# A three-layer graph convolution on one core: every other chunk of layer 1 split for a one-pass product, 18 blocks instead of 16 by count matrices, and an opening that asks for x earlier and holds the first searches

## The chip, the cores and the metric

The kernel runs on one NeuronCore of a Trainium2 chip. A core has engines that run side by side, each taking its own instructions in order: TensorE (PE: matrix products, weight loads listed as PEld), VectorE (DVE), ScalarE (ACT), GpSimd (POOL) and SyncE (SP, which here only issues transfers). Transfers run on 16 DMA engines; SP, ACT and POOL can issue them. The metric is device time in microseconds (us), the median of several runs; before the change it is 2774.49 us.

## The reference

A graph has 6250 nodes with 256 features each (x) and 100,000 edges (src to dst), sorted by dst. Each node also gets an edge to itself. With deg the number of edges that arrive at a node:

```python
dinv = jnp.where(deg > 0, jax.lax.rsqrt(deg), 0.0)
norm_edge = dinv[src] * dinv[dst]
h = x
for W, b in ((W1, b1), (W2, b2), (W3, b3)):      # 256->512, 512->512, 512->256
    agg = segment_sum((h @ W)[src] * norm_edge[:, None], dst, n)
    h = relu(agg + b)
out = layernorm(x + h)
```

Everything is float32. Summing over edges and multiplying by W can change places, and the kernel sums first in layers 1 and 2 (over 256 and 512 columns) and multiplies by W3 first for layer 3 (256 columns).

## The kernel before, in words

**Blocks.** The nodes are cut into NB = 50 blocks of Q = 125. A block's edges lie in a run of the sorted list, about 2000 of them; the kernel loads CAP = 2048 places for each block, 16 for each of 128 partitions (KF = 16). What a block has beyond 2048 goes into a rest, one for each group of GRP = 10 blocks.

**Gathered blocks.** For one chunk (128 edges, one of a block's 16) POOL gathers 128 rows of the layer's table from HBM (L814), by the edges' sources. DVE makes a 0/1 matrix from the edges' targets (L783, for four chunks at once), and PE multiplies matrix and rows (L840) into a sum in PSUM. A float32 product takes two records on PE. Where a chunk is "halved", the row is split first: ACT casts it to the short form fp32r (L855), DVE subtracts that from the row (L858), and high and low part, side by side, go through PE in the short form, twice as wide. Layer 2 halves three chunks of four, layer 3 all but the rests, layer 1 none. SPLIT gives each layer's lags: a row gathered at step c is cast at c + hi_lag, subtracted at c + lo_lag and multiplied at c + lag. The rows lie in a ring of places in one big buffer, room.

**Blocks by matrices (dense).** For the first FEW = 16 blocks of layer 1 and the first MANY = 28 of layer 3 the kernel doesn't gather. It makes the matrix that counts the edges between every source and each of the block's 125 targets, and multiplies it with the whole table, which lies split in SBUF (parts): 50 products of 512 columns a block (L883), after ACT (or DVE) has turned pieces of the matrix from bytes into fp32r (L791). A matrix is made by counts(): for each of 25 groups of 5 targets DVE makes two 0/1 matrices (L684, L686), PE multiplies them (L692), and ACT copies the counts out as bytes (L676) into one buffer, made. SP stores it to HBM (kept) and loads it again (fetch) into one of two buffers, used. The last 12 matrices are made during layer 2. Where the edges of a group of targets begin is found before that by windows(t), a search for 125 groups at a time (t = 0 to 5): comparisons on DVE, two products on PE, one gather by POOL, and transposes, in slots (L614 to L667). Before, all six searches run within layer 1's steps, on a scratch part of room.

**The order of work** is written out by hand. layer() has one step for each gather (548 in layer 1: 34 blocks of 16, and 4 rests; 805 in layer 2; 355 in layer 3, plus lag). A step issues, in this order, a gather, the halving of earlier chunks, the product of an earlier chunk, one advance of every block that is being finished, the fixed extras (searches, counts), and as many dense products as the spacing asks for by then. Finishing (after1, after2, after3) and counts are generators: a number that they yield is how many steps they wait. `first` is the step from which dense products are due, and a dense block may start 10 steps after its matrix was fetched:

```python
until = min(len(dense) * NB, int((chunk + 1 - first) * NB / spacing))
...
if chunk < total - 1 and (len(there) <= m or there[m] > chunk):
    break
```

**Around the layers.** The find stage (L1146 on) loads dst, finds where each block's edges begin and, on ACT's queue, asks for the first two groups of x. The opening of sorted_path then loads the edges (SP 25 blocks, ACT 15, POOL 10), asks for the rest of x, counts degrees in three stages for each of five groups (counted: L499 to L534; DVE, PE, ACT), scales x by dinv on ACT, stores it as layer 1's table (SP), splits it into parts (L542, L543), and loads the weights (late_w, L1127). SP's and ACT's transfers take eight semaphores in turn, so that each waits for the one eight before it.

## Time and profile before

| | |
|---|---|
| runs | 2773.09, 2774.49, 2784.61 us |
| profiled execution | 2775.35 us; span of its instructions 2773.6 us |
| granted PE clock, mean | 0.908 |
| busy: PE, DVE, ACT, POOL | 78%, 52%, 43%, 62% |
| first gather of layer 1 / 2 / 3 | 85.5 / 952.5 / 2190.8 us |
| gathers of layer 1 / 2 / 3 | 548 / 805 / 355 |

The span is the time from the first to the last instruction of one execution. A group of instructions is listed as line, engine, operation, what it writes and reads, and then its busy time, the mean ns of one, and the idle time of its engine ahead of it with what ended it. A list of waits has the waiting instruction, the one that ended the wait, total us, times and the longest. "remote" and "issue" in such a place mean that the profile names no releaser. A row of the timeline has start, duration, engine and line; neighbours are merged, and matmuls overlap, so their pace is read from starts.

### The profile page before, as it was taken

To read this page: it belongs to the slowest core of one execution; us is meant where nothing else is said; L and a number is where in the kernel's file an instruction comes from. 1 tells how busy PE (TensorE), PEld (TensorE's weight loads), DVE (VectorE), ACT (ScalarE), POOL (GpSimd) and SP (SyncE) were. 2 spreads that over 40 slices of the span, in tenths; PEclk is the share of its full clock that TensorE was granted. 3 is DMA by queue.
4 is the path that set the end of the run, shared out by engine and by line. 5 is a ranking of instruction groups with operands and counts; after the bars stand their busy time and mean duration, and the time that the engine had idled before them with its cause. 6 is when DMAs were issued, how large, how long until landed. Compare 5 with 4: busy or idle time off the path is not lost.

```text
span 2773.6 us, 30036 instructions
## 1 busy us (share of the span) xinstructions
PE 2155.2 (78%) x8189; PEld 1492.7 (54%) x8189; DVE 1430.3 (52%) x3657; ACT 1179.0 (43%) x2501; POOL 1716.7 (62%) x1749
## 2 busy tenths in 40 slices
PE   3368877888888768788878777887887679888887
PEld 2246555665566435555545544554555556666664
DVE  5454443444342256556656555565555246556666
ACT  2234444444442244445544443454443245444443
POOL 2565656566666567776767666667766366666663
PEclk9889999999999879999889989998999789999998
DMA  7444545454544466676767667666676355555553
GB/s 177 127 119 136 142 118 152 119 154 123 149 121 133 125 197 197 200 211 196 210 187 212 194 175 214 190 205 192 203 208 195 95 136 148 145 144 154 144 152 95
DMA packets 179311, 450.29 MB, mean 162 GB/s; under 512 B 43801, under 2 KB 75883, under 8 KB 179132
## 3 DMA queue, kind: packets, MB, share of 16 engines
q0 software_dynamic: 108992, 330.44, 42.4%
q1 hardware_dynamic: 53735, 104.78, 13.0%
q10 hardware_dynamic: 16405, 13.06, 1.8%
q8 instruction: 66, 1.08, 0.2%
q14 instruction: 113, 0.93, 0.1%
HBM read 394.24 MB, written 53.88 MB: 162 GB/s over the span
## 4 chain that ended last, share of the span: by engine, by line
PE 35%; issue 13%; DVE 6%; ACT 4%; another core or an unknown queue 3%; DMA 3%; POOL 1%; ACTq 0%; SPq 0%; DVEq 0%; POOLq 0%
PE sacc L840 15%; PE sacc L883 11%; PE win_ps L970 4%; DVE halves L858 3%; ACT halves L855 2%; PE smm L987 2%; DMA room<-tab,ssrc 2%; PE mat_ps L692 1%; POOL room L814 1%; DVE shot L783 1%; PE szt_ps L906 1%; DVE hot_key L686 1%; ACT room L676 1%; ACT piece L791 0%
## 5 line engine op out<-in xcount | busy, mean ns | idle before, releaser
L814 POOL DMA_INDIRECT room<-tab,ssrc x1696 | 1681.5, 991 | 888.4 <-issue 329.4
L858 DVE TENSOR_TENSOR halves<-room,halves 128x512 fp32r<-128x512 f32 (+1 forms) x952 | 556.1, 590 | 617.2 <-issue 280.7
L883 PE MATMUL sacc<-parts,piece 125*125 125x512 f32 x2200 | 758.6, 444 | 61.1 <-ACT piece L791 28.6
L840 PE MATMUL sacc<-halves,shot 128*125 128x512 f32 x1552 | 655.1, 490 | 144.8 <-issue 71.9
L855 ACT CAST halves<-room 128x512 fp32r<-128x512 f32 (+1 forms) x952 | 498.5, 539 | 561.0 <-DMA room<-tab,ssrc 149.6
L840 PE MATMUL sacc<-room,shot 128*125 128x256 f32 (+1 forms) x1700 | 660.7, 477 | 33.8 <-DMA room<-tab,ssrc 32.0
L883 PEld LDWEIGHTS sacc<-parts,piece 125*125 125x125 f32 x2200 | 413.8, 197 | 297.3 <-issue 163.2
L840 PEld LDWEIGHTS sacc<-halves,shot 128*125 128x125 f32 x1552 | 295.9, 204 | 460.2 <-issue 293.9
L676 ACT CAST room<-mat_ps 125x250 uint8<-125x250 f32 x700 | 305.0, 436 | 540.7 <-PE mat_ps L692 211.6
L840 PEld LDWEIGHTS sacc<-room,shot 128*125 128x125 f32 x1700 | 329.9, 202 | 201.4 <-issue 108.5
L692 PE MATMUL mat_ps<-hot_key,hot_lo 128*125 128x250 bf16 x700 | 199.9, 286 | 287.8 <-issue 106.8
L684 DVE TENSOR_SCALAR hot_lo<-keys,slots 128x125 bf16<-128x125 bf16 x700 | 192.9, 276 | 378.8 <-PE mat_ps L692 139.4
L783 DVE TENSOR_TENSOR shot<-near_cols,sdlo 128x500 fp32r<-128x500 f32 (+1 forms) x452 | 302.7, 670 | 103.7 <-PE sacc L840 55.0
L791 ACT CAST piece<-room 125x625 fp32r<-125x625 uint8 x356 | 252.9, 711 | 148.4 <-PE sacc L883 53.4
L970 PE MATMUL win_ps<-room,w_sb 128*128 128x250 f32 x800 | 217.0, 398 | 1.6 <-ACT room L978 0.9
L686 DVE TENSOR_SCALAR hot_key<-keys,slots 128x250 bf16<-128x250 bf16 x700 | 209.7, 300 | 0.0
L970 PEld LDWEIGHTS win_ps<-room,w_sb 128*128 128x128 f32 x800 | 162.8, 204 | 51.9 <-issue 24.2
L692 PEld LDWEIGHTS <-hot_lo 128*125 128x125 bf16 x700 | 101.7, 146 | 85.9 <-issue 34.9
L930 PE MATMUL smm<-w,szt 128*125 128x512 f32 x200 | 108.8, 632 | 7.5 <-issue 6.5
L987 PE MATMUL smm<-w,room 128*125 128x256 f32 x400 | 108.5, 397 | 0.0
L987 PEld LDWEIGHTS smm<-w,room 128*125 128x125 f32 x400 | 79.3, 198 | 26.6 <-issue 12.8
L814 POOL DMA_INDIRECT room<-tab,rest x12 | 14.1, 1178 | 109.1 <-DMA sb<-in_L_gnn_b 57.6
(162 smaller groups left out, 973.0 us busy)
## 6 DMA issues: line engine op xcount, KB each, us to landing
room<-kept SPq DMA_DIRECT2D x44, 683.6 KB
room<-tab,ssrc POOLq DMA_INDIRECT x1696
kept<-room SPq DMA_DIRECT2D x28, 683.6 KB
tab<-st SPq DMA_DIRECT2D x75, 224.0 KB
room<-tab SPq DMA_DIRECT2D x50, 224.0 KB
room<-in_x SPq DMA_DIRECT2D x50, 112.0 KB
out<-st ACTq DMA_DIRECT2D x50, 112.0 KB
room<-in_x ACTq DMA_DIRECT2D x4, 1120.0 KB
```

The source lines that it names most:

```text
L676: nc.scalar.copy(made[:, :, u * G:(u + 1) * G], mat_ps[:Q, u % 2, :G * NB].rearrange("p (k r) -> p k r", r=G))
L686: nc.vector.tensor_scalar(hot_key, keys, slots[:, t, 1, w:w + 1], None, op0=ALU.is_equal)
L692: nc.tensor.matmul(mat_ps[:Q, u % 2, :G * NB], lhsT=hot_lo, rhs=hot_key, start=True, stop=True)
L783: nc.vector.tensor_tensor(hot[:, :n], near_cols.unsqueeze(1).to_broadcast([P, n, Q]), dlo.rearrange("p b j -> p (b j)")[:, at:at + n].unsq ...
L791: convert(piece, used[m % 2][:, c * PIECE:(c + 1) * PIECE, :])
L814: nc.gpsimd.indirect_dma_start(out=row, out_offset=None, in_=tables[i], in_offset=bass.IndirectOffsetOnAxis(ap=at, axis=0))
L840: nc.tensor.matmul(acc[:Q, :size], lhsT=hot, rhs=row[:, c0:c0 + size], start=(i == 1 and k == c0 == 0), stop=(k == KF and c0 + size == row ...
L855: nc.scalar.copy(halves[:, :width], landed[chunk - hi_lag])
L858: nc.vector.tensor_sub(halves[:, width:], landed.pop(chunk - lo_lag), halves[:, :width].bitcast(F32))
L883: nc.tensor.matmul(acc_d[:Q], lhsT=got[done // PIECE][:, k % PIECE, :], rhs=parts[:, k], start=False, stop=(k == NB - 1))
L970: nc.tensor.matmul(h_ps[:, f, :], lhsT=w2_sb[:, k, (f2 + f) * P:(f2 + f + 1) * P], rhs=zt2[:, k, :], start=(k == 0), stop=(k == KH - 1))
L987: nc.tensor.matmul(u_ps[:, h, :], lhsT=ht2[:, k, h * Q:(h + 1) * Q], rhs=w3_sb[:, k, :], start=(k == 0), stop=(k == KH - 1))
```

## The change

1. Layer 1 splits every other chunk (`items[c][2] % 2 > 0`: 8 of 16) with the lags (1, 2, 4), from a new pool of three buffers.
2. FEW goes from 16 to 18: layer 1 gathers 32 blocks, and layer 2 makes 10 matrices instead of 12. Dense products are due from step 28 instead of 52. counts() no longer takes two of its steps in one step of the layer now and then (only the first matrix does, every other time), and its last copy is one step of its loop.
3. The scratch of the searches moves from room to w2's place in SBUF, and layer 1's ring of rows grows from 12 to 19. w2 is loaded at the start of layer 2, ahead of w3, instead of in the opening.
4. The opening: three groups of x instead of two are asked for in the find stage. One group is left to ACT, and SP takes the last group and the zero rows. The first two searches run between the stages of counted and the splitting of x; the other four stay in layer 1.
5. after1 waits two steps more in two places. Layer 3's dense sums use one bank of their own and the two banks of the searches and matrices, instead of three of their own.

windows() itself is unchanged and only stands further up in the file, ahead of the opening that now uses it. The diff, cut to its core:

```diff
-SPLIT = (None, (1, 2, 4), (3, 4, 6))
-FEW = 16
+SPLIT = ((1, 2, 4), (1, 2, 4), (3, 4, 6))
+FEW = 18
...
+    scratch = w2_sb.rearrange("p k n -> p (k n)")
...
-            for g in range(2 * GRP, 4 * GRP, GRP):
-                load_x(nc.scalar, rows_of(room, g), g)
-            load_x(nc.scalar, last_x, NB - GRP)
+            load_x(nc.scalar, rows_of(room, 3 * GRP), 3 * GRP)
+            load_x(nc.sync, last_x, NB - GRP)
             for table in tables:
-                nc.scalar.dma_start(out=table[N:N + 1, :], in_=zero[:, :table.shape[1]])
+                nc.sync.dma_start(out=table[N:N + 1, :], in_=zero[:, :table.shape[1]])
...
+            nc.vector.tensor_copy(thr0, thr_i)
+            nc.vector.tensor_copy(own0, own_i)
+            first_windows = (step for t in range(2) for step in windows(t))
             stages = [counted(g) for g in range(0, NB, GRP)]
             for k in range(NG + 2):
                 for g in range(max(0, k - 2), min(k + 1, NG)):
                     next(stages[g])
+                    if k > 0:
+                        next(first_windows, None)
             nc.vector.tensor_copy(src, ed[:, :, :, 0])
             for g in range(0, NB, GRP):
                 in_parts(g)
+                next(first_windows, None)
+                next(first_windows, None)
+            for _ in first_windows:
+                pass
             late_w()
...
-    scratch = room[:, 3 * MW:3 * MW + 1856]
-    first_rows = [room[:, at:at + C] for at in range(3 * MW + 1856, room.shape[1] - C + 1, C)]
+    first_rows = [room[:, at:at + C] for at in range(3 * MW, room.shape[1] - C + 1, C)]
...
+    split = one.enter_context(tc.tile_pool(name="sfirst_split", bufs=3))
...
+    def dense_bank(i, m):
+        if i < 2:
+            return ps_acc.tile([P, HID], F32, name="sacc")
+        if m % 3 == 0:
+            return ps_dense.tile([P, HID], F32, name="sacc")
+        if m % 3 == 1:
+            return ps_mat.tile([P, HID], F32, name="win_ps")
+        return ps_mat.tile([P, 2, 256], F32, name="mat_ps").rearrange("p t n -> p (t n)")
...
-    def counts(b, rush=GB + 2):
+    def counts(b, rush=GB + 3):
...
-        for u in range(GB + 2):
+        for u in range(GB + 3):
...
-            if u > 1:
+            if 1 < u < GB + 2:
...
-        yield 1
-        moved(GB - 1)
-        yield SOON
         by_rows(nc.sync, made.rearrange("p k v -> p (k v)"), kept[b], store=True)
...
-        hi_lag, lo_lag, lag = SPLIT[i] or (0, 0, 0)
+        hi_lag, lo_lag, lag = SPLIT[i]
...
-            return 0 <= c < total and items[c][1] is not None and (i == 2 or i == 1 and items[c][2] % 4 > 0)
+            return 0 <= c < total and items[c][1] is not None and (i == 2 or items[c][2] % (2, 4)[i] > 0)
...
-                        acc_d = ps_dense.tile([P, HID], F32, name="sacc")
+                        acc_d = dense_bank(i, m)
...
-        yield SOON
+        yield SOON + 2
         yield from transposed(zs, C, got)
...
-        yield SOON
+        yield SOON + 2
         yield from take("mm2", 1)
...
-    seen = 0
+    seen = 2
...
-        for t in range(NW):
-            yield from quick(windows(t)) if t == 0 else windows(t)
+        for t in range(seen, NW):
+            yield from windows(t)
             seen += 1
...
-            yield from counts(b, 5)
+            yield from counts(b) if m else counts(b, 2)
...
-    first = 52
+    first = 28
...
     def last_weights():
+        load_w2()
         load_w3()
         yield 1
...
-    ps_dense = ctx.enter_context(tc.tile_pool(name="sps_dense", bufs=3, space=bass.MemoryType.PSUM))
+    ps_dense = ctx.enter_context(tc.tile_pool(name="sps_dense", bufs=1, space=bass.MemoryType.PSUM))
...
-            for g in range(0, 2 * GRP, GRP):
+            for g in range(0, 3 * GRP, GRP):
                 load_x(nc.scalar, rows_of(room, g), g)
```

## Prediction

> **What bounds the kernel now.** I read the windows first, one for each stage, cut where the gathers (POOL L814) of a layer begin and end. Columns: stretch and length, then busy time (and instructions) of PE, weight loads, DVE, ACT and POOL, the granted clock, DMA share and GB/s.
>
> ```profile
> 85.50:166.00 80.50, 41.99 (x148) 26.67 (x149) 36.11 (x119) 13.02 (x31) 55.24 (x54) 0.86 0.35 99
> 166.00:475.00 309.00, 242.29 (x1032) 176.86 (x1032) 142.31 (x515) 132.04 (x293) 188.20 (x197) 0.93 0.47 133
> 475.00:828.00 353.00, 289.59 (x1214) 211.16 (x1213) 144.31 (x491) 152.96 (x334) 219.14 (x231) 0.94 0.47 136
> 828.00:933.50 105.50, 88.78 (x338) 63.32 (x338) 21.95 (x38) 28.75 (x53) 68.28 (x73) 0.90 0.43 124
> 952.50:2158.00 1205.50, 950.74 (x3314) 606.95 (x3315) 693.16 (x1501) 547.12 (x1111) 823.27 (x804) 0.89 0.68 199
> 2190.00:2748.00 558.00, 469.25 (x1816) 355.01 (x1817) 321.17 (x838) 253.81 (x579) 345.42 (x354) 0.92 0.53 142
> ```
>
> The first four rows are layer 1. It has 548 gathers (34 blocks of 16, and 4 for the rests) in 848 us, 1.55 us a gather. While matrices are made as well as multiplied (166 to 828) a gather takes about 1.56; in the fourth row, where none are made any more, 105.5/73 = 1.45. PE is busy 242.3 + 289.6 = 531.9 of 662 us, 80%. DVE and ACT are at 43%. So PE sets layer 1, with help from waits. Which ones, the list of waits from 85 to 933 us says (total us, times, longest):
>
> ```profile
> ACT room L676 <- PE mat_ps L692: 141.0, 182, 3.2
> ...
> DVE hot_lo L684 <- PE mat_ps L692: 119.2, 148, 6.1
> ...
> POOL room L814 <- PE sacc L840: 69.0, 84, 3.4
> ...
> PE mat_ps L692 <- ACT room L676: 41.1, 34, 10.1
> ```
>
> ACT, DVE and POOL wait for PE (POOL for a row to be free). PE, in turn, waits for other engines mostly ahead of L692, the product that makes the matrices (for ACT 41.1 us, for DVE's hot_key 32.3). The gather itself is not the bound: 0.95 us and 0.30 of issue, 1.25 in all.
>
> **The split of every other chunk in layer 1.** What one product costs is read from starts in the timeline of PE, because neighbours overlap: first layer 1, then layer 3.
>
> ```profile
> 500.32 0.60 PE L840 MATMUL sacc<-room,shot 128*125 128x256 f32 x2
> 500.75 0.27 PE L692 MATMUL mat_ps<-hot_key,hot_lo 128*125 128x250 bf16 x1
> ```
> ```profile
> 2450.14 0.39 PE L840 MATMUL sacc<-halves,shot 128*125 128x512 f32 x1
> 2450.37 1.32 PE L883 MATMUL sacc<-parts,piece 125*125 125x512 f32 x5
> 2451.53 0.39 PE L840 MATMUL sacc<-halves,shot 128*125 128x512 f32 x1
> ```
>
> An unsplit chunk takes two records and 500.75 - 500.32 = 0.43 us; a split one takes one record and 0.23. Five dense products take 2451.53 - 2450.37 = 1.16, also 0.23 each. With 18 dense blocks 32 are gathered, 8 of 16 chunks split: 256 x 0.20 = -51 us of PE. ACT and DVE pay by layer 3's rows for the same shape:
>
> ```profile
> L858 DVE TENSOR_TENSOR halves<-room,halves 128x256 fp32r<-128x256 f32 x352 | 145.5, 420 | 193.5 <-ACT halves L855 98.3 <-issue 86.1 <-ACT piece L791 7.9
> L855 ACT CAST halves<-room 128x256 fp32r<-128x256 f32 x352 | 134.9, 403 | 216.6 <-PE sacc L883 68.8 <-PE sacc L840 48.3 <-remote 41.5
> ```
>
> 256 x 0.403 = 103 us on ACT, 256 x 0.420 = 108 us on DVE. In-order engines: behind the new cast on ACT stand L676 and L791, for which PE waits. The lags leave room: a row gathered at step c is cast at c+1, subtracted at c+2, multiplied at c+4. The lag also adds 4 steps to the end of the layer, 4 x 1.5 = +6 us.
>
> **18 blocks instead of 16.** Two gathered blocks go: 2 x (17 x 0.43 + 0.23) = -15 us of PE, and 32 steps of the layer's loop. Two dense ones come: 2 x 51 x 0.23 = +23.5, and 50 small L692 products, at about 0.12, +6. PE of layer 1 in sum: -51 - 15 + 23.5 + 6 = -36 of 663, so 627/516 = 1.21 us a step, as 663/548 = 1.21 before. **The work per step stays; the steps fall from 548 to 516.** ACT gets 103 + 50 x 0.436 + 20 x 0.71 = 139 more on 327, DVE 108 + 50 x 0.58 - 15 = 122 on 345 (9 us of searches and 6 of L783 go): both become about 466 of 800 us, 58%. Layer 2 shows such a load. While it makes matrices (six stretches together: 271.9 us, 177 gathers, DVE 172.6, ACT 139.6) a gather takes 1.54 at 63% and 51%; between them (292.6 us, 205 gathers) 1.43.
>
> **The pace I take.** The even spread helps: the first dense block moves from step 52 to 28, and in the first row PE was busy 52%, so the 1.56 of the middle came with more than the mean of PE's work; the middle held 423 gathers (428 on POOL less 5 of searches), and 1.21 / (531.9/423) = 0.96 of 1.56 gives 1.50. Matrices are now being made all the time: 27 steps each for a dense spacing of (516 - 40)/18 = 26.4, so from about the sixth block a dense block starts only when its matrix is there, its first piece unconverted (0.71 us on ACT ahead of PE): 12 x 1 us = 12 us, 0.02 a step. The steps that were taken two in one (the rush of 5) and the short waits in after1 go, the 12 rotating rows become 19; ACT and DVE have more in their queues. I take 1.53; the ends are 1.42 (the fourth row, without making) and 1.68 (below). 516 x 1.53 = 789 against 848: **-59**.
>
> Here a rule speaks against the reading. The Trainium skill (Perfetto Trace Analysis, Identifying the Most-Contended Engine) says that matmul busy time is no good measure of how close PE is to its limit, and to take the share of peak arithmetic and the weight loads' busy time. By that row PE has (176.9 + 211.2)/662 = 59%, no bound, and less PE work alone would buy nothing: the loop's steps would count, 32 x 1.55 = -50. By my reading (PE sets it) 848 x 36/663 = -46 before the better spread. Both ends lie close, which is why I trust the size.
>
> **The opening.** Now ACT issues x between the edges and its own roots; DVE stands behind it:
>
> ```profile
> 26.42 9.83 ACTq L54 DMA_DIRECT2D room<-in_x  x4
> 36.29 2.70 ACTq L54 DMA_DIRECT2D last_x<-in_x  x2
> 39.09 3.98 ACTq L556 DMA_DIRECT2D tab<-szero  x3
> 43.16 0.18 ACT L529 ACTIVATE sroot<-sdeg_ps 125x10 f32<-125x10 f32 x1 [35.10 <-DMA room<-in_x]
> ```
> ```profile
> 43.38 0.22 DVE L531 RECIPROCAL sdinv<-sroot 125x10 f32<-125x10 f32 x1 [12.12 <-ACT sroot L529]
> ```
>
> After, ACT issues only one group there, and SP the last group and the zero rows. The 12.1 us wait goes. But (a) the third group of x is 1.25 MB more on ACT's queue, 5 to 7 us at the 177 GB/s and more of the page's first slice, and by the programs' order of waits the fourth edge load of each queue now waits for it: the first 10 blocks' edges, awaited until 19.44, come about 4 us later, and with them the chain to the first reciprocal: DVE itself reaches it at about 36, 7.5 earlier than 43.4. SP's longer queue (its 25 edge loads end at 37.7, some 4 later now, then 5 issues) is done at about 44, before the first stored rows at 45.8. (b) Two searches add 2 x 4.6 us of DVE (rows L614 to L661) and four 1.2 us products with their waits to a loop that took 27 us (43.4 to 70.4). Its waits of 3.23 us for L513 cover some; I count 35, ending at 71. (c) Two steps of the second search stand between the first two subtractions of L543 (+2 us); the rows for gathers now begin in the second group's place, one subtraction (2.8 us) sooner. Sum: 0, from -8 to +8. The searches are then out of layer 1's first steps, which is in the pace. w2 is not loaded here: nothing, since POOL waits for x anyhow.
>
> **Layers 2 and 3.** Ten matrices instead of twelve: 2 x 29 x (1.54 - 1.43) = -6. w2 (1 MB) goes ahead of w3 on SP's queue at step 5, beside gathers that move 199 GB/s: 5 us of all engines' time, +4 with the slack of the rows; its first reader (L970) comes 35 steps later, so nothing waits for it itself. In layer 3 the dense sums use two banks of the matrices instead of two new ones, three in all as before: 0.
>
> **Sum.** 0 - 59 + 6 - 6 + 4 = -55. The profiled execution took 2775.35 (its span 2773.6, 1.7 outside), 0.9 over the runs' median 2774.49; 2775.35 - 55 = 2720, and the median likewise.
>
> **Rivals.** *No gain:* the pace goes to 1.62, so that fewer steps and slower steps cancel: 2720 + 516 x 0.09 = 2766. For it: dense blocks now follow the making of matrices without slack. *Slower:* ACT becomes the bound. Per step it would be busy 466/516 = 0.90, and it now waits for PE at L676 with (141.0 + 104.1)/548 = 0.45 (that row, and its unnamed waits); if these waits don't shrink, and the new casts add 0.2 for rows not yet landed and some 0.06 between instructions, that is about 1.6, and with PE's own wait for late casts 1.68: 2720 + 516 x 0.15 = 2797. It decides from 1.66 on. Against it: layer 2 keeps 1.54 with a fuller DVE. *More gain:* the waits of L692 go with the rush, and layer 1 runs at the 1.42 that layer 2 has between matrices: 2720 - 57 = 2663. Against it: POOL's 1.25 and 18 x 27 steps of making. *The change doing nothing* is excluded for the steps: the built program has 864 gathers of 128x256 instead of 896, and 608 narrow splits instead of 352.
>
> **How the numbers follow.** Likeliest case 0.60 (pace 1.47 to 1.59, 2689 to 2751), more gain 0.13, no gain 0.12, slower 0.15. This kernel's measurement tells 0.5% (14 us) from nothing. Faster 0.74, same 0.11, slower 0.15. Range 2672 to 2782: it leaves out half of the largest gains and most of the slower case.
>
> **What would show it.** First gather at 85 +- 8 us; layer 1's gathers 785 us long at 1.53; L840 with 256 narrow split records more and 620 unsplit; DVE and ACT near 58% there; layer 2 within 10 us of its 1206, layer 3 of its 558. Wrong, if layer 1's step is over 1.6 with ACT or DVE named ahead of L840 or L883; if the opening grows by over 10; if layer 2 loses time at its start to w2.

## The result, and the profile after

The changed kernel takes 2764.88 us (median of 18 runs, 2750.13 to 2777.76) against 2784.01 us for the kernel before (18 runs, 2764.36 to 2797.74). The ratio is 0.994, with a 95% interval of 0.9921 to 0.9958: faster by 0.6%, 17 us by the ratio and 19 by the medians, where 55 were forecast. The two profiled executions lie closer together than the medians: 2775.35 us is below the median of before, 2769.12 (span 2767.1) above that of the changed kernel. So their spans differ by only 6.5 us, and this is where:

| us | before | after | difference | forecast |
|---|---|---|---|---|
| up to layer 1's first gather | 85.5 | 97.1 | +11.6 | 0 (-8 to +8) |
| layer 1, first to last gather | 848.0 (548 gathers) | 833.4 (516) | -14.6 | -59 |
| last gather to layer 2's first | 19.0 | 22.9 | +3.9 | +6 |
| layer 2, to layer 3's first gather | 1238.3 | 1231.0 | -7.3 | -2 |
| layer 3 and end | 582.8 | 582.7 | -0.1 | 0 |

Layer 1 by stretches, as before (stretch and length; busy time and instructions of PE, weight loads, DVE, ACT, POOL; granted clock, DMA share, GB/s):

```profile
97.10:163.00 65.90, 29.90 (x82) 18.59 (x83) 36.84 (x123) 20.15 (x50) 43.45 (x41) 0.96 0.36 103
163.00:475.00 312.00, 233.08 (x941) 163.57 (x941) 162.18 (x563) 154.82 (x377) 179.44 (x186) 0.86 0.44 127
475.00:830.00 355.00, 291.96 (x1177) 202.70 (x1177) 192.79 (x646) 199.45 (x483) 218.39 (x228) 0.93 0.49 139
830.00:930.50 100.50, 83.85 (x326) 59.30 (x326) 45.70 (x134) 50.61 (x118) 62.12 (x65) 0.92 0.49 140
```

The second row has 186 gathers (those of searches included) in 312 us, 1.68 us each; the third has 228 in 355, 1.56. So layer 1 is slow at its beginning. The cut that shows it best is at the 175th step, since the last search in layer 1 ends before it (step 148):

```profile
97.10:405.50 308.40, 206.91 (x792) 143.21 (x793) 160.30 (x555) 135.89 (x331) 177.45 (x179) 0.86 0.42 120
405.50:930.50 525.00, 431.88 (x1735) 300.94 (x1734) 277.20 (x907) 289.15 (x696) 325.94 (x340) 0.93 0.49 139
```

308.4/175 = 1.76 us a step, and then 525/341 = 1.54. Before, the same two numbers were 1.60 and 1.53. At 1.54 the first 175 steps would have taken 270 us: 38 us are lost there (28 against the 280 that they took before). What engines waited for in the first of the two (total us, times, longest):

```profile
ACT room L694 <- remote: 66.7, 13, 12.9
DVE hot_lo L702 <- remote: 49.5, 12, 11.0
POOL w_sb L459 <- DVE hot_lo L702: 41.5, 4, 11.7
```

The third row is new in its size (before, its six gathers waited 21 us in all of layer 1). L459 is the gather of a search, one for each of the four searches that the change leaves in layer 1. It stands in POOL's in-order queue among the rows' gathers, and waits for an index that DVE computes: about 10.4 us each time, in which POOL gathers no row. The first two rows are waits of ACT and DVE whose end the profile can't explain ("remote"); more on them below.

What the new work costs was right. The narrow split took 423 ns on DVE and 404 on ACT (420 and 403 forecast), 256 times more than before:

```profile
L873 DVE TENSOR_TENSOR halves<-room,halves 128x256 fp32r<-128x256 f32 x608 | 254.0, 423 | 348.5 <-ACT halves L870 190.4 <-issue 108.6 <-ACT piece L806 25.6
L870 ACT CAST halves<-room 128x256 fp32r<-128x256 f32 x608 | 239.7, 404 | 246.0 <-PE sacc L855 74.2 <-remote 55.1 <-PE mat_ps L898 30.0
```

The opening, from DVE's timeline (L600 is the reciprocal of one group's roots, L450 reads a search's product from PSUM):

```profile
38.28 0.21 DVE L600 RECIPROCAL sdinv<-sroot 125x10 f32<-125x10 f32 x1
43.54 0.62 DVE L450 TENSOR_SCALAR_CACHE_REDUCE w_sb<-win_ps,w_sb 125x391 f32<-125x391 f32 x1 [5.05 <-PE win_ps L448]
...
75.47 0.62 DVE L450 TENSOR_SCALAR_CACHE_REDUCE w_sb<-win_ps,w_sb 125x391 f32<-125x391 f32 x1 [5.05 <-PE win_ps L448]
...
79.47 0.21 DVE L600 RECIPROCAL sdinv<-sroot 125x10 f32<-125x10 f32 x1
```

The first reciprocal comes 5.1 us earlier than before (38.28 for 43.38) and without its wait of 12.1 us, but the last comes at 79.47 instead of 70.4. DVE's two waits of 5.05 us are for a search's products, which stand on PE behind 30 products for the degrees. The first gather then waits for the third subtraction (L612), not for the second:

```profile
97.13 3.30 POOL L829 DMA_INDIRECT room<-tab,rest  x1 [15.93 <-DVE parts L612]
```

### The profile page after: what moved, and what is told of

Same layout as the page of the kernel before. It is cut to its first block, busy times and chain, and to the rows that moved or that the text cites. A ratio compares the mean times of both kernels' runs of the same rounds, so it can differ in the third digit from the quotient of the medians.

```text
span 2767.1 us, 30455 instructions
## 1 busy us (share of the span) xinstructions
PE 2130.1 (77%) x7965; PEld 1459.2 (53%) x7965; DVE 1512.0 (55%) x3904; ACT 1266.9 (46%) x2777; POOL 1685.0 (61%) x1717
## 4 chain that ended last, share of the span: by engine, by line
PE 53%; issue 17%; DVE 9%; another core or an unknown queue 7%; ACT 6%; DMA 5%; POOL 3%; ACTq 0%; POOLq 0%; SPq 0%; DVEq 0%
PE sacc L855 20%; PE sacc L898 10%; PE win_ps L985 5%; DMA room<-tab,ssrc 4%; PE win_ps L898 4%; PE mat_ps L898 3%; PE mat_ps L710 3%; PE smm L945 3%; DVE halves L873 3%; ACT halves L870 3%; POOL room L829 2%; PE smm L1002 2%; DVE shot L798 1%; ACT piece L806 1%
## 5 line engine op out<-in xcount | busy, mean ns | idle before, releaser
L873 DVE TENSOR_TENSOR halves<-room,halves 128x256 fp32r<-128x256 f32 (+1 forms) x1208 | 663.6, 556 | 805.1 <-ACT halves L870 382.7
L855 PE MATMUL sacc<-halves,shot 128*125 128x512 f32 x1808 | 773.3, 486 | 156.0 <-issue 66.0
L870 ACT CAST halves<-room 128x256 fp32r<-128x256 f32 (+1 forms) x1208 | 600.9, 510 | 610.9 <-PE sacc L855 170.0
L694 ACT CAST room<-mat_ps 125x250 uint8<-125x250 f32 x700 | 305.6, 437 | 544.2 <-PE mat_ps L710 165.4
L898 PE MATMUL sacc<-parts,piece 125*125 125x512 f32 x1400 | 498.7, 454 | 34.5 <-ACT piece L806 19.4
L855 PE MATMUL sacc<-room,shot 128*125 128x256 f32 (+1 forms) x1120 | 483.9, 516 | 10.6 <-DMA room<-tab,ssrc 10.6
L898 PEld LDWEIGHTS sacc<-parts,piece 125*125 125x125 f32 x1400 | 254.8, 203 | 274.0 <-issue 196.4
L798 DVE TENSOR_TENSOR shot<-near_cols,sdlo 128x500 fp32r<-128x500 f32 x443 | 296.3, 669 | 0.1
L855 PEld LDWEIGHTS sacc<-room,shot 128*125 128x125 f32 x1120 | 218.7, 204 | 130.0 <-issue 69.8
L898 PE MATMUL mat_ps<-parts,piece 125*125 125x512 f32 x450 | 132.2, 412 | 16.9 <-ACT piece L806 8.4
L898 PE MATMUL win_ps<-parts,piece 125*125 125x512 f32 x450 | 134.1, 419 | 13.5 <-ACT piece L806 10.3
```

What stands on the lines that cost most here:

```text
L694: nc.scalar.copy(made[:, :, u * G:(u + 1) * G], mat_ps[:Q, u % 2, :G * NB].rearrange("p (k r) -> p k r", r=G))
L798: nc.vector.tensor_tensor(hot[:, :n], near_cols.unsqueeze(1).to_broadcast([P, n, Q]), dlo.rearrange("p b j -> p (b j)")[:, at:at + n].unsq ...
L855: nc.tensor.matmul(acc[:Q, :size], lhsT=hot, rhs=row[:, c0:c0 + size], start=(i == 1 and k == c0 == 0), stop=(k == KF and c0 + size == row ...
L870: nc.scalar.copy(halves[:, :width], landed[chunk - hi_lag])
L873: nc.vector.tensor_sub(halves[:, width:], landed.pop(chunk - lo_lag), halves[:, :width].bitcast(F32))
L898: nc.tensor.matmul(acc_d[:Q], lhsT=got[done // PIECE][:, k % PIECE, :], rhs=parts[:, k], start=False, stop=(k == NB - 1))
```

## The experiments

The experiments ran on five chips, and the chips differ far more than any edit: the kernel before takes 2816 us on chip A and 2782 on chip E, near the 2784 of the measurement above, but 2373, 2377 and 2374 on B, C and D. I call A, E and the chip above the slower chips. A ratio always compares runs of one chip. Beside that I compare lengths only where the kernel before agrees: within B, C and D (0.2%), and more roughly among the slower chips (1.2%). Each length comes from one profiled execution. The column layer 1 runs from its first to its last gather, in us.

| run | kernel | chip | median us | ratio to before (95%) | first gather | layer 1 |
|---|---|---|---|---|---|---|
| e1 | changed, no split | A | 2803.59 | 0.9964 (0.9939 to 0.999) | 96.3 | 828.8 |
| e2 | before, split | A | 2805.52 | 0.9985 (0.9956 to 1.0014) | 88.1 | 856.0 |
| e3 | changed, old opening | A | 2822.53 | 1.0041 (1.0015 to 1.0067) | 88.3 | 865.6 |
| e4 | changed, far searches | A | 2764.00 | 0.9831 (0.9798 to 0.9865) | 96.5 | 798.3 |
| e5 | changed, ring of 12 | B | 2368.86 | 0.9977 (0.9966 to 0.9987) | 99.8 | 692.3 |
| e6 | before, ring of 19 | B | 2375.49 | 1.001 (0.9999 to 1.0021) | 86.1 | 705.0 |
| e7 | far searches, no split | B | 2351.48 | 0.9923 (0.9905 to 0.994) | 97.3 | 667.5 |
| e8 | far searches, 16 blocks | B | 2392.10 | 1.0075 (1.0058 to 1.0092) | 97.6 | 706.5 |
| e9 | changed | C | 2354.62 | 0.9901 (0.9878 to 0.9925) | 96.9 | 668.8 |
| e10 | far searches | C | 2346.75 | 0.9875 (0.9856 to 0.9895) | 97.6 | 667.3 |
| e11 | before, far searches | C | 2374.34 | 0.9989 (0.9977 to 1.0001) | 86.3 | 702.7 |
| e12 | far searches, ring of 12 | C | 2372.64 | 0.9981 (0.9969 to 0.9992) | 97.3 | 687.0 |
| e13 | far, search ahead of the loop | D | 2339.31 | 0.9849 (0.9825 to 0.9874) | 85.8 | 679.1 |
| e14 | e13, other order of x | D | 2334.41 | 0.9838 (0.9814 to 0.9862) | 81.9 | 668.4 |
| e15 | far, old order of asking for x | D | 2343.58 | one run | 95.4 | 667.5 |
| e16 | far, pause between matrices | D | 2388.20 | 1.0063 (1.004 to 1.0085) | 96.4 | 694.9 |
| e17 | as e14 | E | 2716.75 | 0.9779 (0.9736 to 0.9822) | 82.3 | 800.2 |
| e18 | e14, no split | E | 2708.95 | 0.9733 (0.9696 to 0.977) | 81.9 | 786.5 |

### The searches that are left in layer 1

**e4** puts 24 steps instead of 6 between a search's index and its gather ("far searches"), so that DVE has made the index by the time POOL comes to it:

```diff
-        yield LATE
+        yield LATE if t < 2 else 24
         got = scratch[:Q, 816:1072].bitcast(I32).rearrange("p (e t) -> p e t", t=2)
         nc.gpsimd.indirect_dma_start(
```

> The changed kernel, in which the four searches that are left in layer 1 wait 24 steps instead of 6 between the index and their gather, so that POOL, which runs up to 17 rows ahead, need not stand for DVE. If the lost lead of POOL makes the first 175 steps slow, they go from 1.76 to about 1.62 and the time falls 25 us, to about 42 under the kernel before. If the matrices and dense blocks that begin earlier do it, nothing changes: within 8 us of the changed kernel.

Measured: 0.9831, 47 us under the kernel before on that chip (42 expected). The same two stretches of e4's layer 1, in the view of the windows:

```profile
96.50:372.10 275.60, 201.38 (x782) 140.68 (x783) 155.91 (x535) 135.30 (x330) 175.14 (x179) 0.92 0.45 129
372.10:894.80 522.70, 427.35 (x1752) 299.92 (x1751) 281.08 (x928) 289.80 (x699) 327.39 (x342) 0.94 0.48 142
```

The first 175 steps take 275.6 us instead of 308.4, 1.575 a step; the rest is unchanged at 1.53. POOL's four waits fell from 10.4 us to 0.3 each. So the near gathers of four searches had cost some 33 us of layer 1. (The changed kernel itself was not run on chip A; e1, which was, waits 57 us at its four near gathers and takes 315 us for the first 175 steps.)

How they cost it is another matter, and the trace of the changed kernel speaks against the plain answer, that PE ran out of rows. Here are the sums over the four stretches in which POOL stood (127.3 to 137.8, 193.7 to 204.0, 258.4 to 267.3 and 324.3 to 336.0 us), and then over the four runs of gathers, issued one behind the other, that follow them (137.8 to 169.7, 204.0 to 229.3, 267.3 to 291.3 and 336.0 to 358.7 us):

```profile
sum 41.40, PE 35.19 PEld 24.84 DVE 26.10 ACT 24.19 POOL 0.07; mean PE 8.80 PEld 6.21 DVE 6.52 ACT 6.05 POOL 0.02
```
```profile
sum 103.90, PE 53.74 PEld 36.24 DVE 44.17 ACT 32.58 POOL 80.03; mean PE 13.43 PEld 9.06 DVE 11.04 ACT 8.15 POOL 20.01
```

While POOL stood, PE was busy 85% of the time: it worked off the rows gathered before. In the runs behind it was busy 52%, against 82% from step 175 on. 0.30 of 103.9 us is 31 us, nearly all that e4 gives back. So the time was lost not in the wait but behind it, while POOL gathered its lead again. Nor were rows missing then: at 297 us POOL had issued 115 gathers of layer 1, and PE had made fewer than 100 products. Why PE does so little in these runs is not shown; the last section comes back to them.

The length of the waits fits the ring. With 17 rotating rows and the split's lag of 4, POOL runs up to 13 steps ahead of PE, and the gather stands 6 steps behind its index: (13 - 6) x 1.54 = 10.8 us, for 8.9 to 11.7 measured. Without the lag (e1, 17 steps ahead) the same sum gives at most 17, and the waits were 14.0, 14.1, 16.5 and 12.7; before, with 10 rows, it gives at most about 6, and they were 1.3 to 6.6.

**e3** undoes the opening and takes all six searches into layer 1 again. It also has the old start and rhythm of the matrices (`counts(b, 5)`):

```diff
-            for g in range(0, 3 * GRP, GRP):
+            for g in range(0, 2 * GRP, GRP):
                 load_x(nc.scalar, rows_of(room, g), g)
...
-            load_x(nc.sync, last_x, NB - GRP)
+            load_x(nc.scalar, last_x, NB - GRP)
...
-            first_windows = (step for t in range(2) for step in windows(t))
+            first_windows = (step for t in range(0) for step in windows(t))
...
-    seen = 2
+    seen = 0
...
-    first = 28
+    first = 52
```

> The changed kernel with the opening of before: two groups of x asked for early, all six searches within layer 1's steps, dense products due from step 52, two steps in one every fifth time. Split, 18 blocks, 19 rows and the later load of w2 stay. First gather at 85.5 again instead of 97.1. If the early start of matrices and dense blocks is what makes the first 175 steps slow (1.76 us), they take 1.60 as before and the time falls 35 to 40 us below the changed kernel's, some 55 under the kernel before. If searches beside a layer with splits are what slows them, the first 250 steps lose what the opening gains: within 12 us of the changed kernel.

Neither size was met: it is slower than the changed kernel (1.0041 for 0.994). The first gather came at 88.3, but five of its six searches stood 9.5 to 13.7 us each, and the first 250 steps took 1.80 us (changed: 1.69). The early start of the matrices is not what slows the layer, since here it was undone. A search in the layer, with its gather 6 steps behind its index and the long ring, cost more than one in the opening.

**e9, e10 and e11** repeat the comparison on a chip of the other kind: the changed kernel itself, e4's kernel, and the kernel before with e4's edit alone.

> The changed kernel itself, beside the three that follow, on one chip. Two of the chips so far hold many of PE's signals to ACT and DVE back for 1 to 25 us (the kernel before takes 2784 and 2816 us there), one doesn't (2373 us). On a chip that does: 0.6% under the kernel before, POOL's waits at the searches some 10 us each. On one that doesn't: POOL is hardly ever far ahead of PE, its waits at the searches are short, and nothing is lost in the first 175 steps; then the fall from 548 to 516 steps shows at once, 1.3 us a step: 30 to 45 us, 1.3 to 1.9% under the kernel before.

> The searches' gathers 24 steps behind their index, on the same chip as the changed kernel. Where PE's signals are late: 30 us under the changed kernel again, 1.7% under the kernel before. Where they are not: POOL's waits at the searches are short in the changed kernel too, so within 8 us of it.

> The kernel before with nothing but its searches' gathers 24 steps behind their index. Its ring of 12 rows lets POOL run only 10 steps ahead, and its waits at the searches come to 21 us in all. If such a wait costs what it lasts, as in the changed kernel: 13 to 20 us under the kernel before where PE's signals are late, and nothing where they are not. If the later end of the searches delays the matrices: 5 to 15 us over it.

There the changed kernel gains 1.0%, the far searches 1.25% (the intervals overlap), and the edit gives the kernel before nothing (0.9989). e9 waits 1.8 us at one of its four searches and 0.3 at the others, and its layer 1 has hardly a slow beginning, as its windows for the first 175 steps and the rest show:

```profile
96.90:330.90 234.00, 196.16 (x830) 138.54 (x831) 162.88 (x578) 143.96 (x350) 178.02 (x179) 0.98 0.55 158
330.90:765.70 434.80, 396.27 (x1707) 279.85 (x1706) 268.88 (x887) 281.41 (x680) 331.09 (x340) 0.98 0.57 167
```

1.34 and 1.28 us a step: PE keeps up, POOL never waits over 0.3 us for a free row and so builds up no full lead, and the index is there when POOL comes to a search. So the loss of 33 us was seen only on chips on which PE falls behind POOL. My 30 to 45 us for e9 was too much for the 22.5 measured: layer 1 gave 34 (668.8 against 702.7 in e11), but the opening took 11 back.

### What the split is worth

**e1, e7 and e18** take the split out of the changed kernel, of e10's and of e17's; **e2** puts it alone into the kernel before.

```diff
-SPLIT = ((1, 2, 4), (1, 2, 4), (3, 4, 6))
+SPLIT = ((0, 0, 0), (1, 2, 4), (3, 4, 6))
...
-            return 0 <= c < total and items[c][1] is not None and (i == 2 or items[c][2] % (2, 4)[i] > 0)
+            return 0 <= c < total and items[c][1] is not None and (i == 2 or i == 1 and items[c][2] % 4 > 0)
```

> The changed kernel with layer 1's chunks unsplit again (no lag, two records of PE a chunk), everything else as changed. PE sets the steps (my working): 256 x 0.20 us of PE come back, layer 1's 516 steps go from 833 to about 880 us, and the time is 30 us over the kernel before. Steps set it (the share of peak arithmetic, so PE work alone buys nothing): 833 us as with the split, 17 us under the kernel before. The split's work on ACT and DVE is what slows the layer: below 815 us, 35 us or more under the kernel before.

> The kernel before with nothing but the split of every other chunk of layer 1 (34 gathered blocks, lags 1, 2, 4). PE sets the steps: 272 x 0.20 = 54 us of PE less, with 6 us of lag a time some 45 us under the kernel before, layer 1's 548 gathers in about 790 us instead of 848. Steps set it: +6, no difference. ACT and DVE set it: 10 to 30 us over the kernel before.

> The kernel with the searches' gathers 24 steps behind their index, without the split of layer 1. PE sets the steps: 256 x 0.20 us back, 6 us of lag less, layer 1 about 843 us instead of 798 and 45 us slower than with the split. Steps set it, or ACT and DVE take back what PE saves: within 10 us of the kernel with the split.

> The best version without the split of layer 1. My step for the split (256 x 0.20 us of PE that sets the layer) asks for 45 us more than with it. If POOL's gathers set the layer (516 x 1.25 = 645 us, and 667 measured with the split and without it in two calls), the two are within 10 us.

The split does not give the 45 us and more that I expected of it in any of the four pairs. Layer 1 takes 828.8 us without it and 833.4 with it (e1 and the changed kernel), 848.0 and 856.0 (before and e2), 667.5 and 667.3 (e7 and e10), 786.5 and 800.2 (e18 and e17). By the ratios the sign is not settled: e2 can't be told from the kernel before, and e1 not from the changed kernel; e10 is 0.5% better with the split than e7 without it, on two chips, and e7's profiled execution is the shortest of its six runs. e17 and e18 ran on one chip, and there the kernel without the split has the lower median, by 8 us, with intervals that overlap. The whole of layer 1 in the windows, first e7 (no split), then e10 (split):

```profile
97.30:764.80 667.50, 616.58 (x2759) 451.87 (x2760) 351.29 (x1208) 354.87 (x775) 496.88 (x519) 0.99 0.56 164
```
```profile
97.60:764.90 667.30, 592.31 (x2532) 418.28 (x2533) 434.21 (x1463) 424.92 (x1029) 509.11 (x519) 0.98 0.56 164
```

PE's busy time falls by 24 us, DVE's rises by 83 and ACT's by 70, and the layer stays as long as it was. POOL is what sets it on these chips: in e10 509 us busy and 519 times 0.30 us between gathers make 665 of 667, without a single longer wait. In e7 POOL waits now and then for a free row, 16 us in all, but its gathers are shorter: 955 ns each on average, for 979 in e10. That holds for all kernels here: 954 to 959 ns in layer 1 without the split, 965 to 979 with it. So where POOL is the bound, the split takes back on POOL most of what it spares in waits for PE. Why a gather takes longer beside the split is not shown. On the slower chips POOL is not the bound (502 + 156 of e4's 798 us), but taking work from PE didn't help there either: here are e17 (split) and then e18 (none), steps up to 175 and behind it.

```profile
82.30:354.60 272.30, 199.32 (x787) 138.21 (x788) 160.31 (x542) 137.29 (x333) 177.94 (x178) 0.94 0.45 131
354.60:882.50 527.90, 427.83 (x1752) 299.33 (x1751) 283.91 (x942) 289.13 (x697) 329.89 (x343) 0.94 0.48 141
```
```profile
81.90:349.30 267.40, 202.55 (x839) 145.18 (x840) 130.44 (x450) 111.75 (x244) 174.61 (x178) 0.90 0.46 132
349.30:868.40 519.10, 452.39 (x1935) 327.21 (x1934) 228.12 (x782) 243.56 (x531) 325.02 (x342) 0.96 0.49 143
```

e18 has 28 us more of PE's work, and its layer is 14 us shorter in the profiled executions.

**e5, e6 and e12** concern the ring of rows that the split's lag needs:

```diff
-    first_rows = [room[:, at:at + C] for at in range(3 * MW, room.shape[1] - C + 1, C)]
+    first_rows = [room[:, at:at + C] for at in range(3 * MW, room.shape[1] - C + 1, C)][:12]
```

and in the kernel before (e6, with w2 loaded at the start of layer 2 as in the change):

```diff
-    scratch = room[:, 3 * MW:3 * MW + 1856]
-    first_rows = [room[:, at:at + C] for at in range(3 * MW + 1856, room.shape[1] - C + 1, C)]
+    scratch = w2_sb.rearrange("p k n -> p (k n)")
+    first_rows = [room[:, at:at + C] for at in range(3 * MW, room.shape[1] - C + 1, C)]
```

> The changed kernel with layer 1's ring of rows at 12 again instead of 19 (10 that rotate instead of 17). In the changed kernel POOL stands 10.4 us at each of the four searches' gathers (POOL is up to 13 steps ahead of PE, the gather asks for 6: 7 steps of 1.5 us), and then issues up to 22 gathers back to back, in which PE is busy 34 to 48%. If the long back-to-back runs after the wait are the harm, a shorter ring makes wait and run shorter: POOL L459 waits some 4 us instead of 10.4, the first 175 steps go from 1.76 to about 1.65, 15 to 20 us under the changed kernel. If the lost lead is the harm, the lead after the wait is 6 steps with either ring and a smaller ring only adds waits for rows: the same or up to 15 us slower than the changed kernel.

> The kernel before with the scratch of the searches in w2's place, w2 loaded at the start of layer 2, and layer 1's ring at 19 rows: no split, 16 blocks, old opening. If the longer ring turns the searches' gathers into long waits and long back-to-back runs, POOL's waits for DVE at them grow from 3.5 us to about 14 each, the first 250 steps lose 30 to 50 us, and the time is about 35 us over the kernel before. If the ring is harmless: within 10 us of it.

> The searches' gathers 24 steps behind their index and a ring of 12 rows instead of 19. POOL's lead is then 10 - 4 = 6 steps with the split's lag of 4 instead of 13. If rows have to be asked for well ahead of PE, layer 1 loses: 10 to 25 us over the same kernel with 19 rows. If the ring is only a means to long back-to-back runs: the same or up to 10 us faster.

These ran on chips where POOL waits 0.3 to 2.5 us at a search, so they don't tell a lost lead from long runs of gathers, for which e5 and e6 were meant. They tell the ring's worth. With the split, 12 rows instead of 19 cost 20 us of layer 1 (e12 and e10): the lag holds a row 4 steps longer, and POOL waited over 0.4 us 25 times, 30 us in all, where in e10 it never did. Without the lag the longer ring is worth nothing (e6, 1.001). So on these chips the ring repays what the lag takes, and no more.

### What 18 blocks are worth

**e8** is e10's kernel with `FEW = 16`.

> The kernel with the searches' gathers 24 steps behind their index and with the split, but 16 blocks by matrices in layer 1 instead of 18 (548 steps, 12 matrices in layer 2). Steps of 1.54 set layer 1: 32 x 1.54 = 49 us more there and some 6 more in layer 2, the time 50 us over that with 18. PE's work sets it: 2 x 14.7 us of dense products and matrices less, 2 x 5.8 us of gathered products more, layer 1 18 us shorter.

Measured: 19 us over the kernel before on chip B, where e10 is 30 under it on chip C, so 49 apart. Layer 1 takes 706.5 us with 548 steps and 667.3 with 516: 39.2/32 = 1.23 us a step, although PE is busy 604.6 us in the one and 592.3 in the other. Layer 2 is 15 us longer (1100.2 and 1085.2). The gain of the change is here, in steps. The rest of the change, with far searches, loses those 19 us, 11.5 of them in the opening (first gather at 97.6, in e6 at 86.1).

### The opening

**e13** runs one search in the opening instead of two, and its chain up to the gather ahead of the loop; e4's edit applies to the others. **e14** also changes the order in which x is split (the line with `in_parts`); **e15** is e4's kernel with the old order of asking for x (e3's edits of the loads, and the zero rows by ACT).

```diff
-            first_windows = (step for t in range(2) for step in windows(t))
+            first_windows = windows(0)
+            for _ in range(5):
+                next(first_windows)
...
                     next(stages[g])
-                    if k > 0:
-                        next(first_windows, None)
...
-            for g in range(0, NB, GRP):
+            for g in (GRP, 2 * GRP, 3 * GRP, 0, 4 * GRP):
                 in_parts(g)
...
-    seen = 2
+    seen = 1
```

> The far searches, and one search instead of two in the opening, its chain up to the gather ahead of the three-stage loop, where DVE waits 9.6 us for the edges anyway, and its rest between the splitting of x; x asked for early as in the change. The loop then has no search step: if these cost the opening its 11.6 us, the loop takes 27 us instead of 41, the first gather is issued at 84 +- 3 instead of 97, and the time is 10 to 14 us under that of the far searches. If the order of x costs it, the first gather stays at 95 to 98.

> The same, and x is split group by group in the order 1, 2, 3, 0, 4, since the first gathers land in the places of groups 1 and 2. If the first gather waits for the third subtraction only because of the order, it comes 3 to 5 us sooner than in the run without it (about 80); if it waits for the stored table, nothing changes.

> The far searches with the two searches in the opening, but x asked for as before (two groups early, three groups and the zero rows by ACT). One look at the first gather. If the early third group of x were what delays it, it comes at 85 to 88; if the searches do, at 97 or, with ACT's wait of 12 us back, at 100 to 104.

DVE's timeline of e13, and POOL's first gather:

```profile
38.29 0.21 DVE L600 RECIPROCAL sdinv<-sroot 125x10 f32<-125x10 f32 x1
...
68.62 0.22 DVE L600 RECIPROCAL sdinv<-sroot 125x10 f32<-125x10 f32 x1 [1.11 <-ACT sroot L598]
```
```profile
85.77 3.31 POOL L828 DMA_INDIRECT room<-tab,rest  x1 [53.90 <-DVE parts L612]
```

The same loop without search steps takes 30.3 us instead of 41.2, and the first gather comes at 85.8 instead of 97.6 (e10): the search steps within the loop cost the opening its 11.8 us. In e15 the first reciprocal is at 42.9, the last at 77.8 and the first gather at 95.4: with x asked for as before, and the searches in the loop, the opening is 2 us shorter than e10's. So asking for x early moved the first reciprocal but not the end. e14 shows the order of the splitting, 3.9 us (81.9 for 85.8). Of these 12 and 16 us the medians show less: 34 us (e13) and 39 us (e14) under the kernel before, for e10's 30, with intervals of about 5 us to each side; e13 was expected to gain 10 to 14 over e10. In the profiled execution of e13 layer 1 gave all of it back, 679.1 us for e10's 667.3, with the last gather at 764.9 us in both. POOL waited there 13 times, 16 us in all, mostly for PE. That execution is the longest of e13's five, with a granted clock of 0.936 for e10's 0.964, so it doesn't settle how much arrives. e14 has the lowest median of the three, but its interval overlaps both others; e17 shows its kernel on a slower chip.

> The best version so far (far searches, one early search in the opening, x split in the order 1, 2, 3, 0, 4) beside the same without the split, on one chip. 1.6% under the kernel before where PE's signals are in time (39 us); where they are late, 2.0 to 2.3% (the 1.7% of the far searches and 12 us of opening).

Measured there: 2.2% under the kernel before, and 2.7% without the split (e18, the lowest ratio of all).

### The making of matrices

**e16**, on e4's kernel:

```diff
-            yield from counts(b) if m else counts(b, 2)
+            yield from counts(b, 6) if m else counts(b, 2)
+            yield 4
```

> The far searches, with the making of a matrix shortened by four steps (two in one) and four steps of pause after its store, so that ACT's first copy of the next matrix doesn't stand behind the store (ACT waits for kept 4 to 5 us, 11 to 15 times in layer 1). If these waits reach PE: 10 to 25 us under that of the far searches. If they are hidden by the lead of rows and pieces: within 5 us.

Both sizes were missed. ACT's wait for the store fell as meant, from 61.3 us (17 times, in e10) to 16.8 (8 times) over layer 1, and the layer grew by 27.5 us; POOL waited 33 us for PE in it, where in e10 it never waited over 0.4. The edit also puts four steps between a matrix's store and its load, and the last product of a dense block began 10.7 us behind the last gather, where in e10 it began 1.2 us ahead of it. So shorter waits for the store bought nothing here, and the later matrices are the likely cost; the edit changes both at once, so the two are not told apart.

## Why the forecast was right in sign and wrong in size

**"The searches are then out of layer 1's first steps, which is in the pace"** is the step that failed, with 38 of the 49 us between the forecast's 2720 and the profiled 2769. Two of six searches were out; four stayed, up to step 148, which my own part on the code says. I had put the wait of their gathers in POOL's queue at nothing: it was in the trace of before, 1.3 to 6.6 us, small with a short ring, and the change lengthened the ring. What the runs show in its place: waits of 8.9 to 11.7 us, first steps of 1.76 us instead of 1.54, and 33 us back when the gathers stand farther from their index (e4). By which path the waits reach PE stays open: the loss lies in the runs of gathers behind them.

With the near gathers gone layer 1 takes 798.3 us (e4), where the forecast had 789, and from step 175 on the pace is 1.54. That the forecast's 1.53 came out is in part luck. Before, the same steps already took 1.53: the pace did not change, and the terms from which I made it (a more even spread, unconverted first pieces, fewer short waits) were not tested one by one.

**"The opening ... Sum: 0, from -8 to +8"** is the other, +11.6. The edges came 6.5 us later instead of 4, the first reciprocal at 38.3 instead of 36. My 35 us for the loop came out at 41.2. With the old order of x it takes 34.9 (e15, one run), from 42.9 to 77.8: asking for x early moved the start and not the end. What I had missed is that DVE waits for the search's products behind PE's products for the degrees, 5.05 us twice. And the first gather needs the third subtraction, not the second. "If the opening grows by over 10" was one of my own signs of being wrong, and it came.

**"So PE sets layer 1 ... -51 us of PE"** was wrong as a cause, though it left the size alone. Kernels without the split have about the same pace (e1, e7 and e18); PE's busy time fell by 0.1 us a chunk (24.3/256), not by 0.20. The number survived because I took the gain from the steps (work per step the same, 548 to 516) and not from the split. The rule that I set against my reading, the Trainium skill's (Perfetto Trace Analysis, Identifying the Most-Contended Engine), that matmul busy time is no good measure of PE's limit, was the better guide: by it only steps count, -50 us in layer 1, and e8 and e10 are 39 us apart there, 32 steps of 1.23. The sentence "The gather itself is not the bound" holds on the slower chips and not on B, C and D.

**Layers 2 and 3** came out at -7.3 and -0.1 us, for -2 and 0.

**The rivals.** The rival without a gain named a pace of 1.62 and 2766 us; the mean pace was 833.4/515 = 1.62 and the time 2765. Its cause was another: dense blocks that follow the matrices without slack keep 1.54 once the searches are over. The slower one, ACT as the bound, can be excluded behind step 175: ACT is busy 289 of 525 us there, and 136 of 308 before it. (The prediction names layer 1's gathers once as 789 us long at 1.53 and once as 785; its sum gives 789.)

## What to carry to other kernels

An instruction that depends on a slower engine, put into the in-order queue of an engine that runs ahead, makes that engine wait for its whole lead beyond the steps left between (here 7 steps, about 10 us); when a ring is made deeper, or a lag added, count these places again. Such a wait can cost nothing while it lasts and much behind it, so look at the busy time of the other engines in both stretches. Before work is priced on the engine with the longest busy time, see whether the stage's pace is a step's own floor (here the gather's 0.95 + 0.30 us) or a chain of hand-offs: fewer steps gained where this was tried alone (e8), and less work on the busy engine gained nothing clear in either case. Search steps that fill waits of one engine stand behind another's work too (here 5.05 us twice); put them where both are idle, as e13 did ahead of the loop.

## What the runs showed of the hardware

**Chips differ by 17 to 19% on the same kernel.** The kernel before takes 2782 to 2816 us on some chips and 2373 to 2377 on others, and the granted clock of the profiled executions (0.89 to 0.91 against 0.93 to 0.97) is too small a part to explain it: PE's busy time in layer 1 differs by 46 us (638.8 in the changed kernel against 592.4 in e9), the layer's length by 165. What differs in the traces is how soon ACT and DVE go on behind PE. In the changed kernel ACT's copy of a matrix product (L694) came over 1 us behind the product's end, while ACT was idle, 99 times with 273 us in all. Ten of these, 31 us, stand behind the store of the matrix before; the other 89, 243 us, are late behind PE. In e9, the same kernel, all 16 such places (47 us) stand behind the store, and none is late behind PE. The kernel before has 70 late ones with 199 us, so the change did not bring them. A place in the trace of the changed kernel (timelines of PE, ACT and DVE):

```profile
218.78 0.37 PE L710 MATMUL mat_ps<-hot_key,hot_lo 128*125 128x250 bf16 x1 [2.01 <-issue]
...
219.80 0.63 PE L855 MATMUL sacc<-halves,shot 128*125 128x512 f32 x1
224.42 0.37 PE L710 MATMUL mat_ps<-hot_key,hot_lo 128*125 128x250 bf16 x1 [3.99 <-ACT room L694]
```
```profile
223.93 0.44 ACT L694 CAST room<-mat_ps 125x250 uint8<-125x250 f32 x1 [4.63 <-remote]
```
```profile
223.93 0.34 DVE L702 TENSOR_SCALAR hot_lo<-keys,slots 128x125 bf16<-128x125 bf16 x1 [5.18 <-remote]
```

PE ends its last product at 220.4 by the profile, which only models such ends; ACT and DVE both start at 223.93, their waits ended by nothing that the profile names, and PE waits for ACT. In e3 all three stood for 21 to 25 us in this way (PE from 119.9 to 144.7). Meanwhile POOL issued gathers back to back: this place, too, lies in one of the four runs behind a search. But these runs are not the cause by themselves: in the window of 142.4 to 169.7 us both the changed kernel and e9 (second fence) have 22 gathers, with PE busy 9.3 us in the one and 24.8 in the other.

```profile
142.40:169.70 27.30, 9.28 (x28) 5.85 (x28) 10.14 (x35) 6.05 (x16) 20.87 (x22) 0.78 0.54 151
```
```profile
142.40:169.70 27.30, 24.76 (x116) 17.72 (x115) 20.93 (x81) 18.83 (x47) 20.90 (x22) 1.00 0.51 147
```

What holds ACT and DVE back behind PE on some chips, or PE's products themselves, stays open: no record in the trace names it, and no edit here removed it. The pair of runs that was to tell a lost lead from long runs of gathers (e5, e6) fell on a chip without the effect; on a slower chip it would still be worth making.
